# A graph network layer on one core: x's part of the first node layer computed in the first stage, the doubled x through memory, and the division by counts split over two engines

## The chip, the cores and the metric

The kernel runs on one core of a Trainium2 chip. The metric is the device time of one launch in microseconds (us). A core has a matrix engine (TensorE, PE in the profile), a vector engine (VectorE, DVE), a scalar engine (ScalarE, ACT), a general engine (GpSimd, POOL) and a queue engine (SyncE, SP) that here only starts transfers. Each engine works through its own list in order. SBUF is the on-chip memory of 128 partitions, PSUM the small memory that the matrix engine writes to, and DMA transfers move data between SBUF and the device memory.

## What is computed

There are 6250 nodes with 128 features each and 100000 edges that are sorted by destination. An edge's message goes through three layers, the messages of a destination are averaged, and a node network of two layers uses the node's x and that mean. Cut to what matters:

```
h        = relu([x[src], x[dst]] @ Wm1 + bm1)
h        = relu(h @ Wm2 + bm2)
messages = h @ Wm3 + bm3
agg      = segment_sum(messages, dst) / max(count, 1)
upd      = relu([x, agg] @ Wn1 + bn1) @ Wn2 + bn2
out      = layernorm(x + (x + upd))
```

The first node layer can be written as `x @ Wn1[:128] + agg @ Wn1[128:] + bn1`. Its first term needs no edge at all.

## The kernel before, in words

**First stage** (lines 147 to 326). x is loaded in 49 tiles of 128 nodes into `x_sb` (lines 170 to 178). TensorE transposes it into `xT` (`turn`), and multiplies `xT` with the two halves of Wm1 (`products`, line 223). `a_table` writes the source part to a table `atab` in device memory, 1 KB a node; `b_table` splits the destination part into three bf16 terms and writes them to `btab`, 1.5 KB a node. `b_table` for tiles 4i to 4i+3 comes three blocks behind `a_table`, so the last products on TensorE are those of `b_table`. Their PSUM tiles rotate through five buffers (pool `pb`). ScalarE and VectorE empty them; the written rows wait in six SBUF buffers (pool `brow`) for their transfer. TensorE's order is the program's (`manual_schedule`); the order on the other engines is chosen by the scheduler.

**Loop over the edges** (lines 469 to 513). It is written out in full: 196 groups of 512 edges. For a group, POOL gathers 4 x 128 rows of `atab` into `ag` (`fetch`, line 353; four buffers), SP loads four windows of `btab` into `bw` (line 364; four buffers), and ACT's queue loads the destinations into `db` (`destinations`, line 367). VectorE makes the 0/1 matrices `oht` and `oh` (`hot`); TensorE turns the gathered rows and adds the windows' rows (`first_layer`, lines 407 and 413), ScalarE applies the relu (line 418), TensorE multiplies with Wm2 (`second_layer`, line 427), VectorE empties that (line 429), TensorE sums over edges (`sums`, line 436) and VectorE adds the sums of a window into `acc` (`add_up`, line 452). Loads run two groups ahead of `first_layer`, `sums` three groups behind it. `acc` holds, for each node, 256 sums and, in `acc[:, HC]`, the count of edges.

In the loop's groups 20 to 68 VectorE also replaces x_sb by 2x + bn2, one tile of 128 nodes at a time (`double`, line 464).

**Last stage** (lines 553 to 651). Nodes are worked in blocks of 512: first a block of 106, then eleven of 512, and two of 256 at the end. `products(b)` starts `put` with Wn1's x half times `xT` (line 586, two PSUM tiles), makes `pmt` = W3 times the sums (line 590), and `agg` = pmt / count + a constant where the count is not 0: VectorE multiplies by `rc` = 1/count (line 592) and adds `const_part` (line 593), which POOL makes (line 582). For the first two blocks VectorE makes `rc` itself (lines 577, 578); for the rest it comes from a table `rtab` by a transfer that copies it to all partitions (line 580). `hidden(b)` adds Wn1's other half times `agg` to the same `put` (line 601) and ScalarE takes bias and relu (line 602). `norm(b)` multiplies by Wn2 (line 614), adds 2x + bn2 (line 617), normalizes each row (lines 621 to 632) and stores. TensorE's order is `hidden(b)`, `norm(b-1)`, `products(b+2)`.

Of the kernel before, what the change touches and what calls it, by code (L numbers as in the profile page):

```python
# [27 lines left out]
def kernel(  # L28
# [72 lines left out]
    btab = dram.tile([NPAD, 3, H], BF16, name="btab")  # L101
    dpad = dram.tile([NG * GE], I32, name="dpad")
    rtab = dram.tile([NT * P], F32, name="rtab")

    ident = const.tile([P, P], F32, name="ident")
    make_identity(nc, ident)
# [36 lines left out]
    b3 = const.tile([P, 1], F32, name="b3")  # L143
    b23 = const.tile([P, 1], F32, name="b23")
    bu1 = const.tile([P, HC], F32, name="bu1")
    edge = ExitStack()
    ld = edge.enter_context(tc.tile_pool(name="ld", bufs=4, side="right"))

    with tc.tile_pool(name="prep", bufs=1) as prep, tc.tile_pool(
# [28 lines left out]
            nc.sync.dma_start(x_sb[:N - NTF * P, NTF, :], x[NTF * P:, :])  # L178
        nc.sync.dma_start(w2, wm2.rearrange("(k p) h -> p k h", p=P))
        nc.sync.dma_start(w3, wm3.rearrange("(k p) h -> p k h", p=P))  # L180
        nc.vector.memset(xT[:, N:], 0.0)


# [35 lines left out]
        BEHIND = 3  # L219
        INDICES = 6  # L220
        LATE = BLOCKS - 4

        def products(t0, m, k):
            pbt = pb.tile([P, 2, H], F32, name="pbt")
# [76 lines left out]
        for i in range(BLOCKS + BEHIND):  # L301
# [9 lines left out]
            if i >= BEHIND:  # L311
                for t0 in range(4 * (i - BEHIND), min(4 * (i - BEHIND) + 4, NT), 2):
                    b_table(t0)


        PIECE = NPAD // 8
        for c in range(HC + 1):
# [9 lines left out]

    dst_row = dst.rearrange("(o e) -> o e", o=1)  # L330
    late = ctx.enter_context(tc.tile_pool(name="late", bufs=1))
    wu1 = late.tile([P, 2, H], F32, name="wu1")
    wu2 = late.tile([P, HC, D], F32, name="wu2")
    bu2 = late.tile([P, 1, D], F32, name="bu2")

    def late_loads():
        nc.sync.dma_start(wu1, wn1.rearrange("(k p) h -> p k h", p=P))
        nc.sync.dma_start(wu2, wn2.rearrange("(k p) h -> p k h", p=P))
        nc.sync.dma_start(bu2[:, 0, :], bn2.rearrange("(o h) -> o h", o=1).to_broadcast([P, D]))

    with edge, tc.tile_pool(name="wk", bufs=2) as wk, tc.tile_pool(
# [11 lines left out]
        def fetch(idx, nt, firsts):  # L353
# [9 lines left out]
                terms = btab[ds(first, WB + 1)].rearrange("n c h -> (n c) h")  # L363
                nc.sync.dma_start(bw[j // 2 * NQ:(j // 2 + 1) * NQ, j % 2, :], terms[:NQ])
            return ag, bw

        def destinations(g, ng, dst_row=dst_row):

            db = ld.tile([P, 2, 2 * P], I32, name="db", bufs=3)
            if isinstance(g, int) and g < 6:  # L370

                nc.vector.tensor_copy(db[:, 0, :1], srcT[:, 0, :1])
            for h in range(2):
                edges = dst_row[:, ds(g * GE, ng * GE)].rearrange("o (s e) -> o s e", s=ng)
                edges = edges[:, :, h * 2 * P:(h + 1) * 2 * P]
                nc.scalar.dma_start(db[h * NQ:(h + 1) * NQ, :ng, :], edges.to_broadcast([NQ, ng, 2 * P]))
            return [db[:, k, :] for k in range(ng)]

        def last_destinations():
            db = ld.tile([P, 2, 2 * P], I32, name="db", bufs=3)  # L380
# [78 lines left out]
            return list(firsts)  # L459


        x2 = x_sb

        def double(t):
            n = min(P, N - t * P)
            nc.vector.scalar_tensor_tensor(x2[:n, t, :], x_sb[:n, t, :], 2.0, bu2[:n, 0, :],
                                           op0=ALU.mult, op1=ALU.add)

        ahead, lag = 2, 3
        st = {}  # L470
        for i in range(NG + ahead + lag + 1):
            if i == 16:
                late_loads()
                none = wk.tile([16, (NG * GE - E) // 16], I32, name="none", bufs=1)
                nc.vector.memset(none, NONE)
                nc.sync.dma_start(dpad[:E].rearrange("(p e) -> p e", p=16), dst.rearrange("(p e) -> p e", p=16))
                nc.sync.dma_start(dpad[E:].rearrange("(p e) -> p e", p=16), none)
            if 20 <= i < 20 + NT:
                double(i - 20)
            if i < NG:  # L480
                nt = GT if i < NGF else LT
                firsts = load_bases(tilei[0:1, i * GT:(i + 1) * GT], nt, ENG.SP)
                if i == NGF:
                    dbs = last_destinations()
                elif i % 2 == 0:
                    dbs = destinations(i, min(2, NGF - i))
                st[i] = dict(nt=nt, got=fetch(srcT[:, i, :], nt, firsts), db=dbs.pop(0))
            g = i - ahead
            if 0 <= g < NG:
                s = st[g]  # L490
                ag, bw = s.pop("got")
                oht, s["oh"] = hot(s.pop("db"), pbase[:, g, :], dloc[:, g, :s["nt"]], s["nt"])
            k = g - lag - 1
            if 0 <= k < NG:
                s = st.pop(k)
                if "firsts" not in s:
                    s["firsts"] = load_bases(tilei[0:1, k * GT:(k + 1) * GT], s["nt"], ENG.DVE)
                add_up(s["part"], s["firsts"], s["nt"])
            if 0 <= g < NG:
                s = st[g]  # L500
                s["h1"] = first_layer(ag, bw, oht, s["nt"])
            k = g - lag
            if 0 <= k < NG:
                s = st[k]
                s["part"] = sums(s["oh"], s["h2"], s["nt"])
            m = g - 1
            if 0 <= m < NG:
                s = st[m]
                s["h2"] = h2s[m % NH2]
                second_layer(s["h1"], s["h2"], s["nt"])  # L510
            if m == NG - 1:
                for k in range(NG - lag, NG):
                    s = st[k]
                    s["firsts"] = load_bases(tilei[0:1, k * GT:(k + 1) * GT], s["nt"], ENG.DVE)
# [35 lines left out]
    NB = 4 * P  # L550
    NC = NT * P // P

    nodes_of = [(NTF * P // NB * NB, N)] + [(n0, n0 + NB) for n0 in range(0, NTF * P // NB * NB, NB)]
    n0, n1 = nodes_of.pop()
    nodes_of += [(n0, n0 + NB // 2), (n0 + NB // 2, n1)]
    SELF = 2
    with tc.tile_pool(name="nd", bufs=2) as nd, tc.tile_pool(name="nr", bufs=1) as nr, tc.tile_pool(
        name="pm", bufs=2, space=PSUM
    ) as pm, tc.tile_pool(name="pu", bufs=4, space=PSUM) as pu, tc.tile_pool(
        name="po", bufs=2, space=PSUM  # L560
    ) as po, tc.manual_schedule(engines={ENG.PE}):

# [8 lines left out]
        def products(b):  # L571

            n0, n1 = nodes_of[b]
            w = n1 - n0
            rc = nd.tile([P, NB], F32, name="rc", bufs=4)
            if b < SELF:
                nc.vector.tensor_scalar_max(rc[:, :w], acc[:, HC, n0:n1], 1.0)
                nc.vector.reciprocal(rc[:, :w], rc[:, :w])
            else:
                nc.sync.dma_start(rc[:, :w], rrow[:, n0:n1].to_broadcast([P, w]))  # L580
            const_part = nd.tile([P, NB], F32, name="const_part", bufs=3)
            nc.gpsimd.tensor_scalar(const_part[:, :w], acc[:, HC, n0:n1], 1.0, b23, op0=ALU.min, op1=ALU.mult)  # L582
            puts = []
            for c in range(HC):
                put = pu.tile([P, NB], F32, name="put")
                nc.tensor.matmul(put[:, :w], wu1[:, 0, c * P:(c + 1) * P], xT[:, n0:n1], start=True, stop=False)  # L586
                puts.append(put)
            pmt = pm.tile([P, NB], F32, name="pmt")
            for c in range(HC):
                nc.tensor.matmul(pmt[:, :w], w3[:, c, :], acc[:, c, n0:n1], start=(c == 0), stop=(c == HC - 1))  # L590
            agg = nd.tile([P, NB], F32, name="agg", bufs=3)
            nc.vector.tensor_mul(agg[:, :w], pmt[:, :w], rc[:, :w])
            nc.vector.tensor_add(agg[:, :w], agg[:, :w], const_part[:, :w])  # L593
            return puts, agg

        def hidden(b, puts, agg):
            n0, n1 = nodes_of[b]
            w = n1 - n0
            u = nd.tile([P, HC, NB], F32, name="u")
            for c in range(HC):  # L600
                nc.tensor.matmul(puts[c][:, :w], wu1[:, 1, c * P:(c + 1) * P], agg[:, :w], start=False, stop=True)
                nc.scalar.activation(u[:, c, :w], puts[c][:, :w], AF.Relu, bias=bu1[:, c:c + 1])
            return u

        def norm(b, u):
# [1 line left out]
            w = n1 - n0  # L607
            k = -(-w // P)
            r = min(P, w)
            t0 = n0 // P  # L610
            pot = po.tile([P, 4, D], F32, name="pot")
            for i in range(k):
                for c in range(HC):
                    nc.tensor.matmul(pot[:r, i, :], u[:, c, i * P:i * P + r], wu2[:, c, :],
                                     start=(c == 0), stop=(c == HC - 1))
            y = nd.tile([P, 4, D], F32, name="y")
            nc.vector.tensor_add(y[:r, :k, :], x2[:r, t0:t0 + k, :], pot[:r, :k, :])
            st = nd.tile([P, 4, 6], F32, name="st")
            mv = nd.tile([P, 4, 2], F32, name="mv")
            for i in range(k):  # L620
# [16 lines left out]
                nc.sync.dma_start(out[n0:n1, :], o[:r, 0, :])  # L637

        B = len(nodes_of)
        ready = {b: products(b) for b in range(2)}  # L640
        us = {}
        for b in range(B):
            us[b] = hidden(b, *ready.pop(b))
            if b > 0:
                norm(b - 1, us.pop(b - 1))
            if b + 2 < B:
                ready[b + 2] = products(b + 2)
        norm(B - 1, us.pop(B - 1))


# [27 lines left out]
```

## Time and profile before

| what | value |
|---|---|
| median of 3 runs | 1224.58 us (1223.6 to 1225.11) |
| the profiled execution's own time | 1475.88 us |
| its span, first to last instruction | 1474.1 us |
| busy, TensorE / VectorE / ScalarE / POOL | 1248.9 / 646.8 / 440.6 / 814.5 us |
| first stage, until TensorE's first group of edges | 0 to about 70 us |
| loop, until TensorE's last instruction in it | about 70 to 1374 us |
| last stage | 1376 to 1474 us |
| device memory read / written | 162.5 MB / 19.7 MB |

The profiled execution takes 251 us more than the median: to record it costs time, and not equally in each stage. A time of the profile is therefore good for a piece of work, and its sums stand against 1475.88, not against 1224.58. In a line of a timeline the first number is the start from the span's beginning, the second the time that the merged instructions cover; then come engine, source line, operation, tiles as output<-inputs, and how many instructions. A bracket at the end gives the idle time before, and what ended it. "SPq" and "ACTq" are the queues of these engines, which only start transfers. A float32 product appears as two matmul records.

### The profile page before, as it was taken

How to read it: one execution, taken by the hardware profiler on the slowest of the kernel's cores; microseconds unless marked ns; L12 is line 12 of the kernel's file. 1: busy time of each engine (PE TensorE's matmuls, PEld its weight loads, DVE VectorE, ACT ScalarE, POOL GpSimd, SP SyncE). 2: the span in 40 equal slices, each digit the busy share in tenths (PEclk: the TensorE clock that was granted, in tenths of full speed). 3: DMA queues.
4: the chain of work that ended last, by engine and by line, in shares of the span. 5: the costliest groups of instructions: out<-in, count | busy, mean ns of one | idle time of the engine just before them, and what ended most of it. 6: DMA issues, size and time to landing. Idle time of an engine off the chain costs nothing. (4 is left out here: it accounts for less than half of the span.)

```text
span 1474.1 us, 32680 instructions
## 1 busy us (share of the span) xinstructions
PE 1248.9 (85%) x11192; PEld 918.8 (62%) x11193; DVE 646.8 (44%) x2086; ACT 440.6 (30%) x1142; POOL 814.5 (55%) x858
## 2 busy tenths in 40 slices
PE   7748888888888888888888888888888888889897
PEld 6626666666666666666666666666666666666555
DVE  6814443433434434444444444444444444444454
ACT  4512222222222222222222222222222222223244
POOL 7355655556556555655555555565555565563320
PEclk9959999999999999999999999999999999999999
DMA  9845444444444444444444444444444444442121
GB/s 275 288 160 136 119 121 125 120 125 118 118 127 123 120 128 115 121 128 123 120 123 120 122 127 125 119 125 116 123 126 121 124 124 116 124 122 59 47 68 54
DMA packets 158772, 184.06 MB, mean 125 GB/s; under 512 B 30214, under 2 KB 131994, under 8 KB 158588
## 3 DMA queue, kind: packets, MB, share of 16 engines
q0 software_dynamic: 37984, 103.35, 25.6%
q1 hardware_dynamic: 92056, 52.32, 12.1%
q10 hardware_dynamic: 28564, 26.27, 6.4%
q8 instruction: 90, 1.47, 0.4%
q14 instruction: 78, 0.64, 0.1%
HBM read 162.52 MB, written 19.68 MB: 124 GB/s over the span
## 5 line engine op out<-in xcount | busy, mean ns | idle before, releaser
L358 POOL DMA_INDIRECT ag<-atab,srcT x784 | 752.7, 960 | 527.9 <-PE ph L413 318.7
L427 PE MATMUL ph<-w,h 128*128 128x256 f32 x3128 | 735.0, 388 | 0.6 <-issue 0.4
L427 PEld LDWEIGHTS ph<-w,h 128*128 128x128 f32 x3128 | 582.9, 191 | 155.1 <-issue 56.9
L418 ACT ACTIVATE h<-ph,b 128x256 f32<-128x256 f32 x782 | 307.0, 475 | 931.2 <-PE ph L413 827.9
L429 DVE TENSOR_TENSOR h<-ph,nb 128x512 f32<-128x512 f32 x391 | 268.5, 692 | 692.9 <-PE ph L407 353.1
L413 PE MATMUL ph<-oht,bw 64*128 64x128 bf16 x1564 | 126.0, 217 | 188.4 <-issue 163.9
L413 PEld LDWEIGHTS <-bw 64*128 64x128 bf16 x1564 | 67.4, 94 | 232.0 <-issue 186.6
L452 DVE TENSOR_TENSOR acc<-acc,pt 128x63 f32 x782 | 172.2, 220 | 29.6 <-DVE acc L452 1.9
L407 PE MATMUL ph<-ident,ag 64*128 64x64 f32 x3128 | 134.2, 223 | 10.7 <-DMA ag<-atab,srcT 5.1
L436 PE MATMUL pg<-h,oh 128*32 128x257 f32 x1564 | 127.2, 394 | 1.5 <-issue 1.5
L407 PEld LDWEIGHTS ph<-ident,ag 64*128 64x128 f32 x3128 | 114.8, 140 | 10.5 <-DMA ag<-atab,srcT 5.6
L391 DVE TENSOR_SCALAR oht<-db,pbase 128x128 bf16<-128x128 int32 x392 | 104.5, 297 | 23.9 <-PE ph L413 18.5
L447 PEld LDWEIGHTS pt<-ident,part 64*128 64x128 f32 x1173 | 51.0, 136 | 66.7 <-issue 64.3
L439 ACT COPY part<-pg 128x257 f32<-128x257 f32 x196 | 76.8, 392 | 8.0 <-PE pg L436 8.0
L447 PE MATMUL pt<-ident,part 64*128 64x64 f32 x1173 | 77.9, 238 | 1.2 <-DVE acc L452 1.1
L582 POOL TENSOR_SCALAR const_part<-acc,b 128x512 f32<-128x512 f32 (+2 forms) x14 | 24.9, 1777 | 74.6 <-DVE agg L593 44.6
L394 DVE TENSOR_TENSOR oh<-iota_n,dloc 128x128 f32<-128x128 f32 x196 | 55.6, 285 | 5.3 <-PE pg L436 2.8
L226 PE MATMUL pbt<-w,xT 128*128 128x256 f32 x196 | 48.7, 395 | 2.8 <-ACT bt L235 1.9
L436 PEld LDWEIGHTS pg<-h,oh 128*32 128x32 f32 x1564 | 31.3, 108 | 22.9 <-issue 2.2
L226 PEld LDWEIGHTS pbt<-w,xT 128*128 128x128 f32 x196 | 36.5, 196 | 10.6 <-ACT bt L235 3.8
L586 PE MATMUL put<-xT,wu 128*128 128x512 f32 (+2 forms) x56 | 26.0, 590 | 2.8 <-issue 2.6
L246 POOL CAST bt<-rest 128x512 bf16<-128x512 f32 x18 | 12.8, 720 | 27.3 <-DVE rest L244 18.2
(99 smaller groups left out, 388.1 us busy)
## 6 DMA issues: line engine op xcount, KB each, us to landing
bw<-btab SPq DMA_DIRECT2D x782, 32.0 KB
db<-in_dst_dram ACTq DMA_DIRECT2D x194, 128.0 KB
ag<-atab,srcT POOLq DMA_INDIRECT x784
btab<-bt SPq DMA_DIRECT2D x24, 384.0 KB
atab<-bt SPq DMA_DIRECT2D x24, 256.0 KB
out_dram<-o SPq DMA_DIRECT2D x11, 256.0 KB
x_sb<-in_x_dram SPq DMA_DIRECT2D x5, 512.0 KB
rc<-rtab SPq DMA_DIRECT2D x10, 256.0 KB
```

Source lines behind the costliest of these rows:

```text
L226: nc.tensor.matmul(pbt[:, a, :], xT[:, (t0 + a) * P:(t0 + a + 1) * P], w1[:, k, :], start=True, stop=True)
L358: nc.gpsimd.indirect_dma_start(out=ag[:, j, :], out_offset=None, in_=atab[:, :], in_offset=bass.IndirectOffsetOnAxis(ap=idx[:, j:j + 1], a ...
L391: nc.vector.tensor_scalar(oht[:n, k, :], db[:n, k * P:(k + 1) * P], pb_cols[:n, k:k + 1], None, op0=ALU.is_equal)
L407: nc.tensor.matmul(phs[h][:, c, u * NQ:(u + 1) * NQ], ag[halves[h], u, c * P:(c + 1) * P], ident[halves[h], halves[h]], is_transpose=True, ...
L413: nc.tensor.matmul(phs[h][:, c, k * P:(k + 1) * P], bw[halves[h], k, c * P:(c + 1) * P], oht[halves[h], k, :], start=False, stop=True, ski ...
L418: nc.scalar.activation(h1[:, c, h * 2 * P:(h + 1) * 2 * P], phs[h][:, c, :], AF.Relu, bias=b1[:, c:c + 1])
L427: nc.tensor.matmul(ph2[:, a, :], h1[:, c, (j0 + a) * P:(j0 + a + 1) * P], w2[:, c, :], start=(c == 0), stop=(c == HC - 1))
L429: nc.vector.tensor_tensor(h2[:, j0:j0 + 2, :H], ph2, nb2.to_broadcast([P, 2, H]), op=ALU.max)
L436: nc.tensor.matmul(pg[j * WN:(j + 1) * WN, :], oh[:, j, :], h2[:, j, :], start=True, stop=True, skip_group_check=True)
L439: nc.scalar.copy(part[:n, :], pg[:n, :])
L447: nc.tensor.matmul(pt[:, c, :], rows, ident[halves[h], halves[h]], is_transpose=True, start=True, stop=True, skip_group_check=True)
L452: nc.vector.tensor_add(window, window, pts[j // 2][:, :, k:k + WB])
```

## The change

1. Wn1 (`wu1`) is loaded in the first stage, on SP's queue behind Wm2 and Wm3, in place of the late load in the loop.
2. Behind the last `b_table`, TensorE makes x's part of the first node layer for all nodes: 26 products (13 blocks of nodes, two halves of the 256 outputs) into the same five PSUM buffers. ScalarE writes the first half with its bias over `xT`, VectorE the second half over `x_sb`.
3. x is therefore gone from SBUF. In the loop it is loaded again in 13 pieces of up to 512 nodes, doubled and written to a table `x2tab` in device memory; the last stage loads it from there.
4. The orders of VectorE and ScalarE are the program's from here until group 6 of the loop, and the first three loads of destinations stand in the first stage's code.
5. In the last stage `products` has only `pmt`. VectorE makes `total` = acc count x constant + pmt in one operation, and POOL multiplies it by `rc`. `hidden` starts its own `put`; VectorE adds the stored x part, ScalarE takes the relu.
6. The last stage's order is `hidden(b)`, `norm(b-2)`, `products(b+4)` with more buffers for `rc`, `agg` and `u`; the blocks are 106, 256, 256, ten of 512, 256, 256, and VectorE makes `rc` for three of them.

```diff
@@ first stage
         nc.sync.dma_start(w3, wm3.rearrange("(k p) h -> p k h", p=P))
+        nc.sync.dma_start(wu1, wn1.rearrange("(k p) h -> p k h", p=P))
...
+        xu = xT, x_sb.rearrange("p t d -> p (t d)")
...
+        early = [destinations(2 * k, 2, dst_row) for k in range(3)]
+        turns = ExitStack()
+        turns.enter_context(tc.manual_schedule(engines={ENG.DVE, ENG.Activation}))
+        for n0 in range(0, N, 4 * P):
+            n1 = min(n0 + 4 * P, N)
+            parts = []
+            for c in range(HC):
+                pxu = pb.tile([P, 2, H], F32, name="pxu", tag="pbt").rearrange("p t h -> p (t h)")[:, :n1 - n0]
+                nc.tensor.matmul(pxu, wu1[:, 0, c * P:(c + 1) * P], xT[:, n0:n1], start=True, stop=True)
+                parts.append(pxu)
+            nc.scalar.activation(xu[0][:, n0:n1], parts[0], AF.Identity, bias=bu1[:, 0:1])
+            nc.vector.tensor_scalar(xu[1][:, n0:n1], parts[1], bu1[:, 1:2], None, op0=ALU.add)
@@ loop
-            nc.vector.scalar_tensor_tensor(x2[:n, t, :], x_sb[:n, t, :], 2.0, bu2[:n, 0, :],
-                                           op0=ALU.mult, op1=ALU.add)
+            if step == 0:
+                twice[k] = wk.tile([P, 4, D], F32, name="xd")
+                nc.sync.dma_start(twice[k][:r, :n], rows(x))
+            elif step == 1:
+                nc.vector.scalar_tensor_tensor(twice[k][:r, :n], twice[k][:r, :n], 2.0,
+                                               bu2[:r].to_broadcast([r, n, D]), op0=ALU.mult, op1=ALU.add)
+            else:
+                nc.sync.dma_start(rows(x2tab), twice.pop(k)[:r, :n])
...
+            if i == 6:
+                turns.close()
...
-            if 20 <= i < 20 + NT:
-                double(i - 20)
+            for step, after in enumerate((20, 24, 27)):
+                if i >= after and (i - after) % 8 == 0 and (i - after) // 8 < len(pieces):
+                    double((i - after) // 8, step)
@@ last stage
+    full = NTF * P // NB
+    nodes_of = [(full * NB, N)]
+    for k in range(full):
+        cuts = [0, NB // 2, NB] if k in (0, full - 1) else [0, NB]
+        nodes_of += [(k * NB + a, k * NB + b) for a, b in zip(cuts, cuts[1:])]
+    SELF = 3
...
-            const_part = nd.tile([P, NB], F32, name="const_part", bufs=3)
-            nc.gpsimd.tensor_scalar(const_part[:, :w], acc[:, HC, n0:n1], 1.0, b23, op0=ALU.min, op1=ALU.mult)
-            puts = []
-            for c in range(HC):
-                put = pu.tile([P, NB], F32, name="put")
-                nc.tensor.matmul(put[:, :w], wu1[:, 0, c * P:(c + 1) * P], xT[:, n0:n1], start=True, stop=False)
-                puts.append(put)
...
-            nc.vector.tensor_mul(agg[:, :w], pmt[:, :w], rc[:, :w])
-            nc.vector.tensor_add(agg[:, :w], agg[:, :w], const_part[:, :w])
+            nc.vector.scalar_tensor_tensor(total[:, :w], acc[:, HC, n0:n1], b23, pmt[:, :w],
+                                           op0=ALU.mult, op1=ALU.add)
+            agg = nd.tile([P, NB], F32, name="agg", bufs=5)
+            nc.gpsimd.tensor_mul(agg[:, :w], total[:, :w], rc[:, :w])
...
-                nc.tensor.matmul(puts[c][:, :w], wu1[:, 1, c * P:(c + 1) * P], agg[:, :w], start=False, stop=True)
-                nc.scalar.activation(u[:, c, :w], puts[c][:, :w], AF.Relu, bias=bu1[:, c:c + 1])
+                put = pu.tile([P, NB], F32, name="put")
+                nc.tensor.matmul(put[:, :w], wu1[:, 1, c * P:(c + 1) * P], agg[:, :w], start=True, stop=True)
+                nc.vector.tensor_add(u[:, c, :w], put[:, :w], xu[c][:, n0:n1])
+                nc.scalar.activation(u[:, c, :w], u[:, c, :w], AF.Relu)
...
+            x2 = nd.tile([P, 4, D], F32, name="x2", bufs=3)
+            nc.sync.dma_start(x2[:r, :k], x2tab[n0:n1, :].rearrange("(t p) d -> p t d", p=r))
...
-            nc.vector.tensor_add(y[:r, :k, :], x2[:r, t0:t0 + k, :], pot[:r, :k, :])
+            nc.vector.tensor_add(y[:r, :k, :], x2[:r, :k, :], pot[:r, :k, :])
...
+        FORE, BACK = 4, 2
+        aggs = {b: products(b) for b in range(FORE)}
         us = {}
-        for b in range(B):
-            us[b] = hidden(b, *ready.pop(b))
-            if b > 0:
-                norm(b - 1, us.pop(b - 1))
-            if b + 2 < B:
-                ready[b + 2] = products(b + 2)
-        norm(B - 1, us.pop(B - 1))
+        for b in range(B + BACK):
+            if b < B:
+                us[b] = hidden(b, aggs.pop(b))
+            if b >= BACK:
+                norm(b - BACK, us.pop(b - BACK))
+            if b + FORE < B:
+                aggs[b + FORE] = products(b + FORE)
```

## The prediction, as put on record before the changed kernel ran

> **What bounds the kernel now.** I read the page first, then the table by stage, then the timelines of the three places that the change touches.
>
> ```profile
> PE 1248.9 (85%) x11192; PEld 918.8 (62%) x11193; DVE 646.8 (44%) x2086; ACT 440.6 (30%) x1142; POOL 814.5 (55%) x858
> ```
>
> TensorE carries the kernel. The sums by stage say where it does not:
>
> ```profile
> 14.00:72.00 58.00, 51.17 (x255) 41.60 (x253) 45.02 (x82) 34.42 (x64) 27.64 (x38) 1.00 0.88 295
> 72.00:80.00 8.00, 1.53 (x14) 0.97 (x14) 3.08 (x8) 1.62 (x3) 6.17 (x7) 0.50 0.99 351
> 80.00:107.70 27.70, 10.87 (x72) 7.72 (x72) 4.09 (x19) 3.14 (x8) 13.67 (x15) 0.53 0.39 116
> ...
> 1400.00:1420.00 20.00, 20.00 (x83) 11.82 (x82) 10.46 (x37) 9.43 (x20) 5.98 (x3) 1.00 0.28 80
> ```
>
> The columns are stretch, length, busy PE, weight loads, DVE, ACT, POOL, TensorE's clock, DMA share, GB/s. Until 80 the transfers are full (0.88 to 0.99, about 300 GB/s). From 72 to 107.7 TensorE is nearly idle, at half clock. In the last stage it is busy all the time and nobody else is above half. That stage, by block:
>
> ```profile
> 1411.35 1.88 PE L586 MATMUL put<-xT,wu 128*128 128x512 f32 x4
> 1413.07 1.88 PE L590 MATMUL pmt<-acc,w 128*128 128x512 f32 x4
> 1414.78 1.88 PE L601 MATMUL put<-agg,wu 128*128 128x512 f32 x4
> 1416.50 1.95 PE L614 MATMUL pot<-wu,u 128*128 128x128 f32 x16
> 1418.28 1.88 PE L586 MATMUL put<-xT,wu 128*128 128x512 f32 x4
> ```
>
> A block takes 6.93 us with no gap: 1.72 for x's part (L586), 1.71 for pmt, 1.72 for agg's part, 1.78 for pot. VectorE waits in it:
>
> ```profile
> 1411.55 0.69 DVE L617 TENSOR_TENSOR y<-x_sb,pot 128x512 f32<-128x512 f32 x1 [2.01 <-PE pot L614]
> ```
>
> **Profiled and timed run.** The profiled run's own time is 1475.88 (span 1474.1 and 1.8 around it), 251.3 over the median, so I must know where the recording costs. Full groups 1 to 194 start their second layer at 107.74 and 1363.78: 6.51 us apart on average. The last ones, when no gathers or window loads are left, are 5.27 apart:
>
> ```profile
> 1352.67 0.64 PE L436 MATMUL pg<-h,oh 128*32 128x257 f32 x8
> ...
> 1357.94 0.64 PE L436 MATMUL pg<-h,oh 128*32 128x257 f32 x8
> ```
>
> If 5.27 is the timed run's pace, the loop accounts for 193 x 1.24 = 239 of the 251 us. 12 are left, and the loop's start has a candidate, SP's queue:
>
> ```profile
> 79.95 2.92 SPq L364 DMA_DIRECT2D bw<-btab  x2
> 86.47 4.99 SPq L364 DMA_DIRECT2D bw<-btab  x2
> 95.75 4.14 SPq L364 DMA_DIRECT2D bw<-btab  x6
> ```
>
> The first five window loads stand 2.9 to 5 us apart, later ones 0.65 to 0.7. At 0.65 the eight loads of groups 0 and 1 would be out by about 85, not 97.8: some 13 us, about what is left. So I take it that the timed run has no such stall and starts its loop 12 to 13 us earlier. This decides the sum below.
>
> **The change, part by part.**
>
> Last stage, removed: L586 on TensorE. 6250/512 = 12.2 blocks x 1.715 = 20.9 us, all on the path (no gap in 6.93). Left: 1.71 + 1.72 + 1.78 = 5.21 us a block.
>
> Last stage, VectorE. Before: two operations for agg, y, statistics. After: total, two adds of the x part, y, statistics. From start-to-start times around 1411: 0.72 for an operation of 512 columns (L617 to the next), 1.22 for the four pairs of statistics, 0.4 for rs and sh: 4 x 0.75 + 1.2 + 0.4 = 4.6 us a block, under 5.21 but no longer half. A total with three inputs has no row of its own; the nearest, the three-operand L466, takes 284 ns at 128 columns like the two-operand y of one tile (286), so 0.69. While rounds with products last TensorE bounds; the last four rounds have none: TensorE needs 3.5, 3.5, 2.6, 2.6, VectorE 3.9, 3.9, 3.3, 3.3. Its arrears delay the end by about 1 us net. Bounds: nothing, or 3 us.
>
> Last stage, POOL: the multiply of two SBUF tensors is not in the trace. The nearest row is what it replaces there, const_part, 1994 ns at 512 columns. [...] agg is made four blocks ahead; cost 0 either way. [...] If POOL took 5.2 it would bound. ScalarE: relu 2 x 0.69, 0.3, 4 x 0.39 = 3.3 a block, hidden.
>
> Last stage, SP: 15 loads of x2 (3.2 MB). Each stands behind the store of four blocks earlier, which waits for ScalarE's o, and is needed two blocks (10 us) later; hidden. Without that cover, each would cost a landing: a 32 KB window load took 2.3 us (79.95 to 82.28), so 3 to 4 for 256 KB. The start (rc for 106 + 256 + 256 columns, 4.1 us of reciprocals by the 3.3 us of 512) replaces 106 + 512; four products lie ahead. Cost 0, at most 2. Last stage in all: 20.9 - 1.1 = 19.8 us less (16 to 21).
>
> Loop. Removed: 49 doublings of 284 ns; added: 13 of 0.69. VectorE is under half busy: 0. Added on SP: 13 loads and 13 stores of 256 KB among groups 7 to 43, 26 x 0.47 = 12 us of issuing in some 36 x 5.27 = 190; the group's five issues take about 2.9 of 5.27. The store waits for VectorE, with the next groups' window loads behind it, but it stands two to three groups after its load, and windows are buffered over four groups. VectorE's first doubling waits for its load, with add_up and an emptying of ph2 behind it: some 2 us once, within VectorE's slack. I take 0; above, 26 times the 0.87 us that 256 KB takes at 300 GB/s would be 23 if no buffer covered it, but they do: up to 3.
>
> First stage. wu1's 0.26 MB at 300 GB/s, transfer bound: +0.9. The 26 products: 24.4 blocks' halves x 0.857 = 20.9 us of TensorE. They cannot start at 68.3, when b_table's products end:
>
> ```profile
> 63.87 4.42 PE L226 MATMUL pbt<-w,xT 128*128 128x256 f32 x18 [0.36 <-ACT bt L235]
> ```
>
> Their five PSUM buffers are freed by the rest operations at 69 to 74.7. The order on the engines after the change puts ScalarE's and VectorE's first evictions between the last btab pieces, so the last rest moves from 74.3 to about 75.8 and the fifth product waits for it. I get two products by 72.3, two by 74.1, the next two by 77.9, twenty more in 16: 94, with wu1 94.7. Evictions (0.69 each on two engines) keep up with 1.71 a pair. The last btab piece is ready at 79 instead of 75.6; its window loads follow at about 82 instead of 80, hidden under TensorE's new work. PSUM goes over to the loop after the last eviction: group 0 starts at 95.8, its layer ends at 96.9; group 1 waits for ScalarE's 1.57, ends at 99.5; second layer (0) 3.65, at full clock; group 2 waits 0.7 more, since VectorE now makes its oht behind the emptying of ph2. Second layer (1) starts at about 105.
>
> Before, in the timed run without the stall: windows of group 1 land at about 87.2, second layer (0) starts at 87.7, the first part at half clock, second layer (1) at about 94.9. So the first stage costs 105 - 94.9 = 10.1 us.
>
> The clock decides a little here. In the trace it fell to 0.50 at 72.0. [...] By the row, half from 72 on, the products would take up to 41.8 us[...]. In the trace 5.8 busy us (100.4 to 106.2) brought full clock back[...]: cost 1, inside 10.
>
> **Sum.** 1224.6 - 19.8 + 10.1 + 0 = 1214.9, taken as 1215. Against the profiled run's own time, where the stall covers the first stage's new work, it is 1475.9 - 19.8 - 0 = about 1456.
>
> **Rivals.**
> 1. The stall at the loop's start is in the timed run too. Then windows arrive at about 100 either way, and the products lie in a hole: 1224.6 - 19.8 = 1205 (1202 to 1209). For it: the trace shows the stall. Against: the 12 us that the loop leaves over.
> 2. The last stage gives less: VectorE at 4.6 of 5.21 in order, with ScalarE and POOL in each chain, runs at 5.9 a block. 12.2 x 0.7 = 8.5 lost: 1223 (1219 to 1226). Against: in-order waits of before (rs for sd, 0.42) lie under it.
> 3. Slower: the first stage has no hole in the timed run. If its transfers run faster unrecorded and the windows are there when b_table ends, the products stand in the path whole: 20.9 + 0.9 + about 2.5 of handing over = 24.3, against 19.8: 1229. It decides from 20 us of exposure on, that is, if the loop could have begun before 75. Against: btab's writes fill the transfers to 80.
> 4. The change doesn't do what it says: excluded, TensorE's list of the changed kernel has the products ahead of the loop and none in the last stage.
>
> **How the numbers follow.** Likeliest 0.60: 1215 (1211 to 1219). Rival 1: 0.20. Rival 2: 0.12. Rival 3: 0.08. The range 1204 to 1224 holds the first, most of rival 1 and over half of rival 2. Two in a thousand (2.4 us) is about what a measurement can tell: faster than 1222.1 are the first two and a little of rival 2, 0.84; within, 0.08; slower, rival 3 and the end of rival 2, 0.08.
>
> **What would show it.** Last stage: blocks of 5.2 us, no L586 in it, and about 78 instead of 98 us; 6 would be rival 2. First stage: 26 products of two records from about 70.5 to 95, clock 1.00 behind 76; with window loads that land later than 95 the profile shows the stall again, and then profile and timed run part: about -20 in the first, -10 in the second. Second layer (1) at 105 to 110. Groups 7 to 43 as long as the others. Wrong would be all this if the loop's pace changed.

## The result, and the profile after

| | before | after |
|---|---|---|
| median | 1224.39 us (4 runs, 1223.6 to 1225.11) | 1215.34 us (4 runs, 1215.17 to 1216.15) |
| ratio to before, 95% interval | | 0.9927 (0.991 to 0.9945) |
| span of the profiled execution | 1474.1, and 1221.5 when recorded again | 1213.4 us |
| second layer (1) to second layer (194) | 6.51 us a group, and 5.27 | 5.27 us a group |

The kernel is 0.73% faster, 9 us, and 1215.3 is the forecast 1215. Second layer (1) is TensorE's product with Wm2 for group 1 of the loop, and so on. The first profile of before was no measure of the timed runs: recorded once more (run 1 below), the same kernel took 1223.26 us, so I compare the profile after with that second one. The text ahead of the prediction and the prediction itself had put the 251 us down to the recording; that was wrong, and the last section says what it probably was.

The page's first line, of run 1 and then of the changed kernel:

```profile
PE 1180.5 (97%) x11192; PEld 896.5 (73%) x11193; DVE 661.4 (54%) x2086; ACT 439.9 (36%) x1142; POOL 810.6 (66%) x858
```

```profile
PE 1181.3 (97%) x11196; PEld 898.6 (74%) x11197; DVE 675.1 (56%) x2085; ACT 446.8 (37%) x1158; POOL 804.7 (66%) x859
```

TensorE's busy time is the same, and so is the number of products but for two (11196 and 11192 records, two to a product): the work was moved into idle time, not removed. (x's part has 26 products for 28, while pmt and agg's part have two more each, since the last stage has 15 blocks for 14.) The table by stage (stretch, length, busy PE, weight loads, DVE, ACT, POOL, TensorE's clock, DMA share, GB/s) shows where they went:

```profile
72.00:80.00 8.00, 7.22 (x17) 3.15 (x17) 6.26 (x11) 4.42 (x8) 6.31 (x6) 1.00 0.97 335
80.00:107.00 27.00, 23.74 (x129) 14.58 (x128) 9.73 (x27) 9.60 (x20) 15.69 (x17) 0.87 0.48 133
...
1160.00:1180.00 20.00, 20.00 (x96) 12.83 (x95) 16.37 (x52) 11.05 (x25) 5.09 (x4) 1.00 0.32 91
```

In 72 to 80, where TensorE had worked 1.53 us (in both profiles of before, at a clock of 0.50 in the first), it now works 7.22 at a clock of 1.00, while the transfers go on at 335 GB/s. In the last stage VectorE is at 16.4 of 20 us; it was at 10.5. The last stage by TensorE's timeline:

```profile
1167.83 1.88 PE L618 MATMUL pmt<-acc,w 128*128 128x512 f32 x4
1169.55 1.88 PE L632 MATMUL put<-agg,wu 128*128 128x512 f32 x4
1171.27 1.95 PE L645 MATMUL pot<-wu,u 128*128 128x128 f32 x16
1173.05 1.88 PE L618 MATMUL pmt<-acc,w 128*128 128x512 f32 x4
```

A block takes 5.22 us from start to start and has no bracket, that is, no idle time. The price of this stands at the end of the first stage, in the same view:

```profile
70.36 1.98 PE L342 MATMUL pxu<-xT,wu 128*128 128x512 f32 x4 [1.97 <-DVE rest L248]
73.12 19.58 PE L342 MATMUL pxu<-xT,wu 128*128 128x512 f32 x48 [0.78 <-ACT xT L344]
...
96.97 1.48 PE L424 MATMUL ph<-ident,ag 64*128 64x64 f32 x16 [2.57 <-ACT h L435]
...
98.80 5.87 PE L444 MATMUL ph<-w,h 128*128 128x256 f32 x16
...
106.12 3.72 PE L444 MATMUL ph<-w,h 128*128 128x256 f32 x16
```

The 26 products are L342, from 70.36 to 92.7, with one wait of 0.78 in them; the first layer of group 0 follows at 93.42 and ends at 94.4. Two things in these lines were not foreseen: the wait of 2.57 us for ScalarE, and second layer (0), the first L444, which takes 5.87 us where the next takes 3.72.

### The profile page after: what moved, and what is told of

Same layout as the page of the kernel before. It is cut to its first block, busy times and chain, and to the rows that moved or that the text cites. A ratio compares the mean times of both kernels' runs of the same rounds, so it can differ in the third digit from the quotient of the medians.

```text
span 1213.4 us, 32800 instructions
## 1 busy us (share of the span) xinstructions
PE 1181.3 (97%) x11196; PEld 898.6 (74%) x11197; DVE 675.1 (56%) x2085; ACT 446.8 (37%) x1158; POOL 804.7 (66%) x859
## 5 line engine op out<-in xcount | busy, mean ns | idle before, releaser
L444 PE MATMUL ph<-w,h 128*128 128x256 f32 x3128 | 729.7, 386 | 0.0
L444 PEld LDWEIGHTS ph<-w,h 128*128 128x128 f32 x3128 | 579.7, 190 | 151.8 <-DVE acc L469 69.9
L424 PE MATMUL ph<-ident,ag 64*128 64x64 f32 x3128 | 130.6, 223 | 2.9 <-ACT h L435 2.6
L430 PE MATMUL ph<-oht,bw 64*128 64x128 bf16 x1564 | 76.5, 217 | 0.7 <-DVE oht L408 0.7
L623 POOL TENSOR_TENSOR agg<-total,rc 128x512 f32<-128x512 f32 (+2 forms) x15 | 16.0, 1069 | 68.1 <-DMA rcol<-acc 31.6
L430 PEld LDWEIGHTS <-bw 64*128 64x128 bf16 x1564 | 53.7, 96 | 1.1 <-issue 0.9
L645 PEld LDWEIGHTS pot<-wu,u 128*128 128x128 f32 (+1 forms) x196 | 24.0, 191 | 5.5 <-issue 4.8
```

What stands on the lines that cost most here:

```text
L424: nc.tensor.matmul(phs[h][:, c, u * NQ:(u + 1) * NQ], ag[halves[h], u, c * P:(c + 1) * P], ident[halves[h], halves[h]], is_transpose=True, ...
L430: nc.tensor.matmul(phs[h][:, c, k * P:(k + 1) * P], bw[halves[h], k, c * P:(c + 1) * P], oht[halves[h], k, :], start=False, stop=True, ski ...
L444: nc.tensor.matmul(ph2[:, a, :], h1[:, c, (j0 + a) * P:(j0 + a + 1) * P], w2[:, c, :], start=(c == 0), stop=(c == HC - 1))
```

## The experiments

The changed kernel's own median is 1215.34; runs 1 to 4, 5 to 7, 8 to 10, 11 and 12 each stood beside runs of the kernel before on the same chip, whose medians were 1224.57, 1224.34, 1224.01, 1450.58 and 1224.3. These were five different chips.

**1. The kernel before, recorded again.** No edit.

> The kernel before, unchanged, recorded once more. Theory (the recording slowed the first profile of before; the timed run has no stall of SP's queue at the loop's start): where the recording does not disturb, groups are 5.27 us apart, the second layer of group 1 starts at about 94.9 us, and the span is about 1223 us. Rival 1 (the stall belongs to the kernel): that second layer starts at 107 to 108 again even where groups are 5.27 apart.

It took 1223.26 us. Its timelines of TensorE and of SP's queue give the start of the loop:

```profile
86.36 0.50 PE L413 MATMUL ph<-oht,bw 64*128 64x128 bf16 x5 [1.55 <-DMA bw<-btab]
...
95.22 3.72 PE L427 MATMUL ph<-w,h 128*128 128x256 f32 x16
```

```profile
80.12 28.01 SPq L364 DMA_DIRECT2D bw<-btab  x36
```

The 36 window loads leave in one run, 0.78 us apart, without the stalls of 3 to 5 us. Second layer (1) starts at 95.22, where the prediction had worked out 94.9. Second layer (194) starts at 1112.14, so a group takes (1112.14 - 95.22)/193 = 5.269 us. Rival 1, the stall in the timed run, falls. From second layer (194) to the end it is 1221.5 - 1112.14 = 109.4 us.

**2. The changed kernel without the 26 products.**

```diff
-        xu = xT, x_sb.rearrange("p t d -> p (t d)")
+        xu = xT, xT
...
-        for n0 in range(0, N, 4 * P):
...
-            nc.scalar.activation(xu[0][:, n0:n1], parts[0], AF.Identity, bias=bu1[:, 0:1])
-            nc.vector.tensor_scalar(xu[1][:, n0:n1], parts[1], bu1[:, 1:2], None, op0=ALU.add)
```

> The changed kernel without the 26 products of x's part and without their evictions; xT stands in for both halves of the result, so the output lacks x's part of the first node layer. Everything else is as in the changed kernel. Theory (the first stage has a hole that covers about half of the new work, 10.1 us are exposed, +-2): 1215.3 - 11 = about 1204.5 us, second layer of group 1 at about 95. Rival 1 (hole covers all): 1215. Rival 3 (all exposed): 1191 to 1194.

1205.77 us, ratio 0.9848 (0.9834 to 0.9861), 9.6 us under the changed kernel. TensorE's timeline:

```profile
97.09 3.72 PE L434 MATMUL ph<-w,h 128*128 128x256 f32 x16
```

Second layer (1) starts at 97.09 in place of 106.12. So 20.9 us of products cost 9.0 in the trace and 9.6 in the times; the rest lay in the hole of 72 to 86. Of the 9.0, 6.6 are the products that overhang the hole: the first layer of group 0 ends at 94.40 with them and at 87.77 without. The other 2.4 arise behind it: 1.3 in the wait for ScalarE (2.57 for 1.24) and 1.1 in second layer (0) (5.87 for 4.80). Rival 3, products wholly exposed, falls. And 1.9 us (97.09 against 95.22, one trace each) of the first stage's price have nothing to do with the products.

**3. The kernel before without x's part in the last stage.**

```diff
-                nc.tensor.matmul(put[:, :w], wu1[:, 0, c * P:(c + 1) * P], xT[:, n0:n1], start=True, stop=False)
...
-                nc.tensor.matmul(puts[c][:, :w], wu1[:, 1, c * P:(c + 1) * P], agg[:, :w], start=False, stop=True)
+                nc.tensor.matmul(puts[c][:, :w], wu1[:, 1, c * P:(c + 1) * P], agg[:, :w], start=True, stop=True)
```

> The kernel before without its x part in the last stage: the 26 products of Wn1's first half are left out there, agg's products start the sum; nothing else changed. Theory (the last stage is bound by TensorE, 1.715 us a block of 512 are on the path): 1224.4 - 20.9 = 1203.5 us, blocks 5.2 us apart; at worst 2 to 3 us less gain, since this order has one block less of slack. Rival 2 (other engines take over below 6.9): blocks of about 5.9 us, 1212 us.

1204.32 us, ratio 0.9843 (0.9829 to 0.9857). Its last stage by TensorE's timeline:

```profile
1156.84 1.88 PE L589 MATMUL pmt<-acc,w 128*128 128x512 f32 x4
...
1162.06 1.88 PE L589 MATMUL pmt<-acc,w 128*128 128x512 f32 x4
```

The old order, the old buffers and the old division, and again 5.22 us a block. (The 14 blocks of this kernel had 28 products of x's part, not 26.) From second layer (194) to the end it is 89.8 us here and 89.7 in the changed kernel. So the last stage's whole gain is the work taken from TensorE; the new distances, the smaller blocks and the split division cancel in sum. Up to TensorE's last product it is 81.3 us here, with a wait of 1.20 for agg in the first block, and 80.0 in the changed kernel; from there to the end it is 8.5 here and 9.8 there.

**4. The moved multiply on VectorE.**

```diff
-            nc.gpsimd.tensor_mul(agg[:, :w], total[:, :w], rc[:, :w])
+            nc.vector.tensor_mul(agg[:, :w], total[:, :w], rc[:, :w])
```

> The changed kernel with the multiplication by 1/count on VectorE instead of POOL, 15 operations, nothing else. Theory from the prediction (VectorE would pass TensorE, 5.4 us a block instead of 5.21): about 2.4 us slower, 1217.7. From the trace after, where VectorE is busy 82 to 85% of the last stage, less: 0.7 more on 4.3 to 4.4 is 5.0 to 5.1 a block, so 0.5 to 2 us slower, most of it at the end, where VectorE bounds. Rival (POOL and its extra handover cost something themselves): equal or faster than 1215.3.

1216.29 us, ratio 0.9932 (0.9919 to 0.9946), not to be told from the changed kernel's 0.9927. From the table by stage, the stretch 1144 to 1196, first of the changed kernel, then of this one:

```profile
1144.00:1196.00 52.00, 52.00 (x241) 33.85 (x240) 41.05 (x135) 29.87 (x66) 14.44 (x13) 1.00 0.46 141
```

```profile
1144.00:1196.00 52.00, 51.95 (x235) 32.88 (x233) 45.63 (x146) 28.30 (x64) 0.00 (x0) 1.00 0.44 136
```

VectorE rises from 41.05 to 45.63 us of 52, still under TensorE's 52. It doesn't become the bound, the block stays at 5.22, and from second layer (194) to the end it is 89.9 us for 89.7.

**5. The old distances of the last stage.**

```diff
-        FORE, BACK = 4, 2
+        FORE, BACK = 2, 1
```

> The changed kernel with the last stage's order set back to products two blocks ahead and norm one block behind. My theory: TensorE alone sets the last stage once x's part is gone (the kernel before without x's part had the same 5.22 us a block in the old order), so the distances buy nothing: 1215 to 1216.5, blocks of 5.2 us, the last group's second layer to the end at about 90 us. Rival: the longer chain of the changed kernel (VectorE's total, POOL's multiply at 1.27 us, VectorE's add of x's part, ScalarE's relu) needs the longer distances: then TensorE waits in each block, 0.3 to 1 us in each of 12, 1219 to 1227.

1213.49 us, ratio 0.9911 (0.9897 to 0.9925). The interval overlaps the changed kernel's; the block stays at 5.22 and the time is in any case not worse, so the rival (longer chains need longer distances) falls. The spans differ by 1.3 us. The last row of TensorE's timeline, first of the changed kernel, then of this run, shows that it is not TensorE:

```profile
1202.48 1.16 PE L645 MATMUL pot<-wu,u 128*128 128x128 f32 x8 [0.40 <-DVE y L650]
```

```profile
1203.49 0.94 PE L645 MATMUL pot<-wu,u 128*128 128x128 f32 x6 [0.33 <-ACT u L634]
```

TensorE is done later here, at 1204.43 for 1203.64. But from there to the end of the span it is 7.7 us for 9.8: with norm one block behind, VectorE has one y left to begin (seen in run 8, which has the same distances: at 1200.52, 1.41 us behind TensorE's end), with two blocks behind it has two (at 1204.58 and 1207.16). The stage's beginning gives nothing. agg's first product comes 3.2 us earlier (1139.49 for 1142.69), since two blocks of pmt stand ahead of it and not four, but the other two follow later, and agg's first two products take 1.03 us here and 0.59 in the changed kernel, whose clock was 0.50 until 1140.8.

**6 and 7. One block of x's part behind the first layer of group 0; two more behind the last sums of the loop.** The idea was to fill the wait of 2.57 us, and waits at the loop's end.

```diff
+        LATER = {0: 11 * 4 * P, NG - 2: 10 * 4 * P, NG - 1: 9 * 4 * P}
...
                 s["h1"] = first_layer(ag, bw, oht, s["nt"])
+                if g == 0:
+                    x_part(p2, "ph2", "ph2", LATER[0])
...
                 s["part"] = sums(s["oh"], s["h2"], s["nt"])
+                if k >= NG - 2:
+                    x_part(p2, "ph2", "ph2", LATER[k])
```

`x_part` is the loop body of the first stage as a function; run 6 has only the first of the three.

> The changed kernel with the two products of one block of 512 nodes moved from the first stage to the place behind the first layer of group 0, where TensorE waited 2.57 us for ScalarE's first relu and where its clock then fell to half from 96.36 to 103.19 us. My theory: the two products (1.7 us) fill the wait, [...] second layer (0) takes 3.65 us instead of 5.87: 1215.3 - 1.7 - 2.2 = about 1211.4. Rival: the clock falls anyway, or ScalarE's eviction of the moved product delays the relu that TensorE waits for, by up to 0.7: then the gain is 1 to 1.7 only, 1213.5 to 1214.5, or nothing.

> The same as the run with one block behind the first layer, and two more blocks' products moved to the end of the loop, behind the sums of the last two groups, where TensorE was sparse and its clock at half from 1134.0 to 1140.8 us. My theory: the first stage gets 2 x 1.7 = 3.4 us shorter, and at the end of the loop the products lie partly in TensorE's waits: 1206 to 1210. Rival: the loop's end is set by TensorE in order, so that the 3.4 us come back there: equal to the run with one block moved, within 1 us.

Run 6: 1210.4 us, ratio 0.9882 (0.9867 to 0.9897). Run 7: 1209.24, ratio 0.9879 (0.9864 to 0.9894). TensorE's timeline of run 6:

```profile
92.58 1.98 PE L344 MATMUL ph<-xT,wu 128*128 128x512 f32 x4
94.49 0.71 PE L429 MATMUL ph<-ident,ag 64*128 64x64 f32 x16
...
96.13 3.72 PE L449 MATMUL ph<-w,h 128*128 128x256 f32 x16
```

The wait is gone, second layer (0) takes 3.72 (TensorE's clock is 1.00 from 86 to 107), and second layer (1) starts at 101.29, 4.8 us earlier (expected were 1.7 + 2.2). But ScalarE's list had changed as well, as its timeline shows: the first relu now started at 92.72, right behind the first layer, and a load of destinations that had stood ahead of it came at 95.83. So run 6 changed two things, and I could not put its gain down to the filling. Run 7's further 1.2 us in the medians are within the intervals; its span is 2.3 shorter (1207.7 against 1210.0). At second layer (194) it was 3.9 ahead (1115.74 for 1119.62), so 1.6 of it came back behind that, where the two moved blocks now stand.

**8 and 9. Run 7 with the old distances, and then with three buffers for y and o.**

```diff
-        FORE, BACK = 4, 2
+        FORE, BACK = 2, 1
...
-            y = nd.tile([P, 4, D], F32, name="y")
+            y = nd.tile([P, 4, D], F32, name="y", bufs=3)
```

The same edit was made to `o`; run 8 has only the distances.

> The kernel with three blocks moved, with the last stage's old distances (products two blocks ahead, norm one behind). My theory from the run with the old distances alone: fewer products stand at half clock before the first agg, and no later wait eats that up, so the gain of about 1.3 us in the span adds to the other: 1207.3 to 1208.3. Rival: the 1.8 us between the medians of that run and of the changed kernel are chance, then 1209 to 1209.5.

> The same, and y and o of the last stage with three buffers in place of two, since VectorE's last y waited 1.34 us for ScalarE's o of an earlier block. My theory: that wait stands in the chain that ends last, so the end comes 0.5 to 1.3 us sooner: 1206 to 1207.5. Rival: ScalarE's and VectorE's own work sets the tail and the wait only turns into another: within 0.3 us of the run without it.

Run 8: 1209.38 us, ratio 0.9881 (0.9864 to 0.9897), which does not tell it from run 7; only its span is 0.9 shorter. The reason expected, products at half clock, is not what the trace shows: as in run 5, TensorE is done later (1199.11 for 1197.88 in run 7) and what follows is shorter (7.7 us for 9.8). Run 9: 1207.61, ratio 0.987 (0.9853 to 0.9886), the best median of all versions that compute everything. VectorE's last y in run 8, and then in run 9:

```profile
1200.52 0.42 DVE L659 TENSOR_TENSOR y<-x,pot 128x256 f32<-128x256 f32 x1 [1.60 <-ACT o L674]
```

```profile
1198.90 0.42 DVE L659 TENSOR_TENSOR y<-x,pot 128x256 f32<-128x256 f32 x1 [0.23 <-PE pot L654]
```

The wait of 1.60 us for a buffer became 0.23 for the product, and from TensorE's last product to the end it is 1.2 us less (7.7 and 6.5). The medians agree in direction, with overlapping intervals.

**10. Run 2 with Wn1 loaded in the loop.**

```diff
-        nc.sync.dma_start(wu1, wn1.rearrange("(k p) h -> p k h", p=P))
...
+            if i == 12:
+                nc.sync.dma_start(wu1, wn1.rearrange("(k p) h -> p k h", p=P))
```

> The kernel without the 26 products of x's part (its output lacks that part, the last stage adds xT in its place), with Wn1's load put back into the loop, at group 12. It splits the 1.9 us by which second layer (1) came later there than in the kernel before. My theory: the load of 0.26 MB costs the transfer-bound first stage 0.9 us at 300 GB/s and the rest, about 1, is the new order of VectorE and ScalarE: second layer (1) at about 96.2 and a time of 1204.9. Rival: all 1.9 is the order, then nothing changes: 1205.8; or all is the load: 1203.9.

The times are inconclusive: 1207.17 us (1204.93 to 1207.62), ratio 0.9863 (0.9846 to 0.9879), above run 2's median with overlapping intervals. The trace does not settle it either. Second layer (1) starts at 95.65, 1.4 us earlier than in run 2 and 0.4 later than in run 1; 0.33 of the latter is TensorE's wait for oht ahead of it. But `b_table`'s last product, which stands ahead of all that differs in the order, ends at 67.9 (run 1) and 68.4 (here) without the load, and at 68.1 (run 12), 68.4 (changed kernel) and 68.9 (run 2) with it. That scatter is as large as what was looked for. How the 1.9 us divide between the load and the new order stays open.

**11 and 12. The first relu ahead of the fourth load.** The program's order is kept for one group longer.

```diff
-            if i == 6:
+            if i == 7:
                 turns.close()
```

> The changed kernel with one order undone: ScalarE's list had the fourth load of destinations (a buffer that VectorE's masks of groups 0 and 1 must first set free) ahead of the first relu of group 0; the program's order is now kept for one group more, which puts that load behind the relu of group 3. My theory: the relu waited for this load (it began at 95.71, the first layer's last product was done at about 94.4), so TensorE's wait of 2.57 us becomes about 1.25 as in the kernel before, and with the shorter wait the clock stays full and second layer (0) takes 3.65 in place of 5.87: second layer (1) at 102.5 to 103, 1215.3 - 1.3 - 2.2 = 1211.8. Rival A: the wait shortens but the clock falls all the same: 1214. Rival B: the load was not what the relu waited for: unchanged, 1215.3.

> The same kernel as in the run before, whose chip held the loop of every kernel, the kernel before's too, to a slower pace (1450.6 us for the kernel before, nothing recorded). Its trace answered for the wait: 1.32 us in place of 2.57; TensorE's clock still fell, but for 3.4 us in place of 6.8, and second layer (0) took 4.56. On a chip with the usual pace I expect the same there: 1.25 us from the wait and 1.3 from the clock, 1215.3 - 2.6 = 1212.7 (1212 to 1214), second layer (1) at 103.5. Rival: second layer (0) takes what it took in the changed kernel, then 1214.

Run 11 took 1434.76 us beside 1450.58 of the kernel before on the same chip, ratio 0.9891 (0.9873 to 0.9909). Run 12: 1212.96, ratio 0.9911 (0.9897 to 0.9924), expected 1212.7. The interval overlaps the changed kernel's, so the trace has to decide. ScalarE's timeline, first of the changed kernel, then of run 12:

```profile
94.63 0.60 ACTq L328 DMA_DIRECT2D db<-in_dst_dram  x1
95.71 0.47 ACT L435 ACTIVATE h<-ph,b 128x256 f32<-128x256 f32 x1 [2.47 <-DVE oh L411]
```

```profile
93.84 1.57 ACT L435 ACTIVATE h<-ph,b 128x256 f32<-128x256 f32 x4 [1.23 <-PE ph L430]
```

In the changed kernel the relu follows a load that ScalarE issues at 94.63, and the profile puts its wait down to VectorE. The buffer that the load will overwrite is read by VectorE's oht, the last of which (group 1) ends at 94.60; then the load goes out, and the relu behind it. TensorE's product for this relu was done at 94.4. In run 12 the relu is released by the product alone. What TensorE makes of it in run 12, at a clock of 1.00 from 87.57 to 101.21:

```profile
95.10 1.08 PE L424 MATMUL ph<-ident,ag 64*128 64x64 f32 x16 [1.32 <-ACT h L435]
...
96.33 3.72 PE L444 MATMUL ph<-w,h 128*128 128x256 f32 x16
...
101.67 3.72 PE L444 MATMUL ph<-w,h 128*128 128x256 f32 x16
```

The wait is 1.32 as in the kernel before (1.25), second layer (0) takes 3.72, and second layer (1) starts 4.5 us earlier, 0.6 of which came from a first stage that happened to be earlier (L342 at 69.74). Of this 3.5 is left at second layer (194), 1120.17 for 1123.69, and 2.7 at the end: the last stage's first pmt products, 16 records, took 6.95 us in run 12 and 6.19 in the changed kernel, whose clock was 0.50 from 1134.0 to 1140.8. Run 12 has all 26 products in the first stage and still brings second layer (1) to 101.67, run 6 to 101.29. Without the 0.6 that is 3.8 us of run 6's 4.8: most of run 6's gain was the order of ScalarE's list, not the filled wait. My theory for run 6 does not stand as it was put.

## Why the prediction was right, point by point

- **The last stage** was forecast at 19.8 us less, and the span from second layer (194) to the end went from 109.4 to 89.7: 19.7. Its two terms are right as well: up to TensorE's last product 20.85 us less (100.80 to 79.95; forecast 20.9), from there to the end 1.2 more (8.6 to 9.8; forecast about 1 for VectorE's arrears). The block is 5.22 (forecast 5.21), and run 3 shows the cause. Rival 2, 5.9 us a block, did not occur: VectorE was at 79% of 1144 to 1196, 4.1 us in 5.22 where 4.6 had been worked out. (Before, it was not below half, as said, but just above: 10.46 of 20.)
- **The loop** was forecast at 0. The pace went from 5.269 to 5.272, 0.6 us in 193 groups. The 13 pieces through memory cost nothing that can be seen.
- **The first stage** was forecast at 10.1 and cost 106.12 - 95.22 = 10.9. That the two numbers are near is in part luck, for several terms were off in both directions. The products were done 2 us earlier than worked out (92.7 for 94.7). The wait for ScalarE was priced at its own work, 1.57, and lasted 2.57, since the prediction did not look at what ScalarE's list held between its last eviction and its first relu: a load that waits for VectorE, whose masks of groups 0 and 1 the change had put behind its own last eviction. In the kernel before that load was out at 81.39, five us ahead of the relu. Second layer (0) was priced at full clock, 3.65, and took 5.87 at a clock of 0.50 until 103.19. Run 12 shows that the load's place made the wait long (1.32 without it). It does not show the same of the clock, which stayed full in run 12 but fell in run 11 with the same wait of 1.32. The wait of group 2 for oht was 0.33, not 0.7. Wn1's load, priced at 0.9, lies in 1.9 us that run 10 did not divide. By run 2 the 10.9 are 6.6 of overhang, 1.3 of wait, 1.1 of second layer (0) and these 1.9.
- **The clock** did not fall at 72, where the prediction had put 1 us for it (the author's estimate; it was 1.00 from 72 to 80). It fell at 96.36, where none was foreseen. The table by stage, of the changed kernel, of run 11 and of run 12:

```profile
92.70:96.36 3.66, 1.34 (x28) 1.08 (x27) 2.09 (x14) 1.19 (x4) 1.65 (x2) 1.00 0.14 41
96.36:103.19 6.83, 6.22 (x34) 4.98 (x35) 0.51 (x1) 2.48 (x7) 5.31 (x6) 0.50 0.65 173
```

```profile
94.79:98.20 3.41, 1.73 (x32) 1.44 (x30) 2.32 (x14) 2.18 (x6) 1.22 (x1) 1.00 0.18 50
98.20:101.62 3.42, 3.33 (x28) 2.75 (x28) 0.00 (x0) 0.15 (x1) 2.77 (x3) 0.50 0.49 133
```

```profile
90.98:94.39 3.41, 2.44 (x34) 1.86 (x32) 2.48 (x14) 1.48 (x4) 0.61 (x1) 1.00 0.13 37
94.39:97.80 3.41, 2.61 (x31) 2.21 (x32) 0.00 (x0) 2.43 (x7) 2.52 (x3) 1.00 0.45 117
```

  In the changed kernel the clock fell within TensorE's wait of 2.57 us and was 0.50 for 6.8 us, in which TensorE was busy for 6.22. In run 11 it was 0.50 for 3.4 us, behind a wait of 1.32; in run 12, on another chip, it was 1.00 behind a wait of the same 1.32. What decides between these was not shown.
- **The multiply on VectorE** was priced at 2.4 us: 0.8 more on VectorE, so 5.4 a block, 0.2 over TensorE's 5.21, in 12.2 blocks. Run 4 gives 0.95 in the medians, with overlapping intervals. The step that was off added the times of single operations, 5.4 us a block; by the table VectorE was busy 45.63 of 52, 4.6 in 5.22. On POOL the multiply took not the 2.0 us of the nearest row but 1.27, where the kernel before's multiply of pmt by rc took 0.69 on VectorE (L592, 512 columns), and it costs nothing there:

```profile
1170.65 1.27 POOL L623 TENSOR_TENSOR agg<-total,rc 128x512 f32<-128x512 f32 x1 [3.95 <-DVE total L620]
```

- **The reading of the first profile** was right where it counted (a pace of 5.27 and no stall in the timed runs) and wrong in its cause. ("Nearly idle" from 72 to 107.7 was strong, too: the two rows hold 12.4 us of TensorE's work in 35.7.) That the profile would gain 20 us and the timed run 10 did not come to pass, since the profile after was taken at the timed pace.

The sum by the traces: -19.7 + 10.9 + 0.6 = -8.2, and the spans say 1213.4 - 1221.5 = -8.1. The medians say -9.0; the recorded execution of before was 1.1 under its median.

## What to carry to other kernels

Work that moves from a stage where its engine is busy to one where it waits is paid for by what overhangs the hole: here 6.6 of 20.9 us, and 2.4 more behind the hole, 1.3 by a wait and 1.1 by second layer (0), for most of which the clock was 0.50. Where a change fixes an engine's order, read each list at the seam, DMA issues included, and ask for each what releases it: a load for group 6 ahead of the first relu cost some 3.8 us up to second layer (1), more than everything that the change does in the loop. A single experiment that fills a wait may also reorder another engine; look at that engine before the gain is given a name. And where two spans differ, follow the difference to the last instruction: in run 5 a product that came 3.2 us earlier gained nothing, and the gain lay behind TensorE's last one.

## What was not expected of the hardware

The loop did not have the same pace on every chip. Beside run 11, eleven unrecorded runs of the kernel before had a median of 1450.58 us, on a chip other than those of runs 1 to 10 and 12, where the medians were 1224.0 to 1224.6. In run 11 second layer (1) and (194) started at 110.86 and 1346.32, 6.40 us a group for 5.27. SP's queue shows the slower pace, 24 window loads in 34.96 us (32 in 39.52 in run 1):

```profile
603.45 34.96 SPq L393 DMA_DIRECT2D bw<-btab  x24
```

Four such loads go with each group, so this line does not say what sets the pace; that was not tried. One chip, seen once, does not tell the chip from the moment either.

The first profile of before looks the same: 6.51 us a group, and TensorE busy for 1248.9 us, where run 11 has 1249.0 and run 1 has 1180.5. So it is likely that it came from such a chip; which one it was is not known, and 25 us between 1475.88 and 1450.58 stay open. That recording costs time is not seen: the recorded executions of runs 1 and 11 took 1223.26 and 1438.34 us, the unrecorded ones beside them 1223.65 to 1226.45 (the same kernel) and 1431.96 to 1438.52.

Some of the change's new work should be hidden where the loop stalls: run 11 gained 15.8 us there and run 12, the same kernel, 11.3 elsewhere, but the intervals of the ratios (0.9873 to 0.9909, 0.9897 to 0.9924) overlap.
